# hT of two blocks in one tile and one load, loads earlier than the rows, and lists of four blocks in 16 pieces

## The chip, the cores and the metric

The kernel runs on one core of a Trainium2 chip. The metric is the device time of one execution in microseconds, lower is better. A core has five engines with a queue of instructions each: TensorE (PE in the profile, its weight loads PEld), VectorE (DVE), ScalarE (ACT), GpSimd (POOL) and SyncE (SP), which here only issues DMAs. The DMAs of all of them run on 16 DMA engines.

## The reference, cut to what matters

```python
# x: (16, 1024, 256); adj: (1024, 1024), sparse, some 9 nonzeros in a column; D = 256
pre_u = einsum('bud,dk->buk', h_t, W1[:d])
pre_v = einsum('bvd,dk->bvk', h_t, W1[d:])
hidden = relu(pre_u[:, :, None, :] + pre_v[:, None, :, :] + b1)
S = sigmoid(einsum('buvk,ko->buvo', hidden, W2)[..., 0] + b2[0])
a_t = einsum('buv,bud->bvd', S * A_a, h_t)
m_t = einsum('uv,bud->bvd', A_m, h_t) * h_t
z_t = beta1 * h_t + beta2 * (a_t @ Wa + ba) + beta3 * (m_t @ Wm + bm)
```

Both A_a and A_m are `adj`. Only edges (u, v) with a nonzero weight count, so the kernel builds lists of edges and gathers the rows of their sources.

## The kernel before, in words

**Tables and blocks.** The 16 batches are four groups g of GB = 4, and the 1024 nodes are eight tiles of 128. A block (g, vt) is one group and one tile of target nodes, so there are 32. For each group a table in DRAM has a row of 2048 numbers for each node: the four pre_u of the group, then its four h. `rows(k)` makes the first half for one tile of nodes: in two pieces TensorE multiplies hT, the transposed h, by W1's upper half (L384), ScalarE copies the product to `tab` (L400), and one step later SP stores it (L403). `copy_h` (L378) copies h itself from DRAM to DRAM. All rows of a group must be there before the first block of the group gathers.

**Lists.** `lists(vt)` makes the edges of a tile of targets: it loads 128 columns of adj (L238), turns nonzeros to keys (L244), takes the largest keys by maxima (L251 to L260), distributes the edges to slots with small matmuls (L270, L307), and matches slot and edge (L315 to L321). It ends with `uidx`, the sources to gather, `vidx`, where their weights lie, and `onehot`. It is a generator, and each `yield` is a place where it may be put off. The lists of tiles 0 to 3 are made mainly in the opening. Those of 4 to 7 (EARLY = 4) are advanced by the table `advance` while other blocks run. `fetch_val` (L341) then gathers the weights, two gathers of ten a step.

**The main loop.** A block has T = 10 steps, of 128 edge slots each, and the loop over n has 320. `fetch` (L453) gathers a slot's rows, one megabyte if all slots are used, into one of NF = 5 buffers, and is issued up to five steps ahead. `expand` (L523) brings pre_v to the slots with a 0/1 matrix. `gate` adds both (L539, 128x1024) and makes four relu-weighted sums (L543); ScalarE takes the sigmoid (L546) and scales the one-hot matrix with it (L549). `aggregate` (L560) sums h over edges on TensorE. At fixed steps s within a block, `half_end`, `turn_over` (L578, L581, L591) and `block_end` (L609 to L615) finish the block before, and `halves` prepares pre_v of the next one (L384, L420). VectorE's `times_h` (L591) is the last reader of a block's hT.

**Order.** The schedule is written by hand: every engine runs its instructions in the order in which the loop emits them. Blocks run in the order (0, 0..5), (1, 0..5), (0, 6..7), (1, 6..7), (2, 0..7), (3, 0..7). Rows of tiles 6 and 7 of groups 0 and 1 are needed long before their blocks, so their hT is loaded for the rows, given up, and loaded once more (`again`). The rows of the first eight blocks in `turn` are made in the opening; for others `plan` gives three steps each: that of the load and of the copy of h, and those of the two pieces of `rows`:

```python
plan([(2, vt) for vt in range(NT)], ((62 + 10 * i, 68 + 10 * i, 73 + 10 * i) for i in range(NT)))
```

**Buffers.** `hts` has ten buffers of 4 KB a partition, one for each block's hT; `hta` has three more, for blocks that are loaded twice. A load waits on SP's queue until its buffer's last reader is done. SP's queue also carries loads of h (L714), table stores (L403) and output stores (L615), in the order of the loop.

Of the kernel before, what the change touches and what calls it, by code (L numbers as in the profile page):

```python
# [7 lines left out]
FP = mybir.dt.float32  # L8
# [3 lines left out]
ALU = mybir.AluOpType  # L12
AX = mybir.AxisListType
P = 128
# [3 lines left out]
def kernel(  # L18
# [42 lines left out]
    nc = tc.nc  # L61
    B, N, D = x.shape
    NT = N // P
    DC = D // P
    GB = 4
# [21 lines left out]
    xT_rows = xT.rearrange("b (c p) n -> p (b c) n", p=P)  # L87
# [17 lines left out]
    def fixed(shape, name, dt=FP):  # L105
        return const.tile(shape, dt, name=name)
# [5 lines left out]
    ukey = fixed([P, N], "ukey")  # L112
# [96 lines left out]
    main = ctx.enter_context(ExitStack())  # L209
    gat = main.enter_context(tc.tile_pool(name="gat", bufs=1))  # L210
    one = main.enter_context(tc.tile_pool(name="one", bufs=1))
    big = main.enter_context(tc.tile_pool(name="big", bufs=2))
    hts = main.enter_context(tc.tile_pool(name="hts", bufs=NT + 2))
    hta = main.enter_context(tc.tile_pool(name="hta", bufs=3))
    wk = main.enter_context(tc.tile_pool(name="wk", bufs=3))
    psc = main.enter_context(tc.tile_pool(name="psc", bufs=2, space=bass.MemoryType.PSUM))
# [13 lines left out]
    EARLY = 4  # L230
# [3 lines left out]


    def lists(vt):
        key = fetched[vt + 1][:, :N] if vt < EARLY else big.tile([P, N], FP, name="key", bufs=1)
        (nc.sync if 2 <= vt < EARLY else nc.gpsimd).dma_start(key, adjT[vt * P:(vt + 1) * P, :])  # L238
        yield
# [1 line left out]
        top = R[:, 5:5 + S]  # L241
        count = wk.tile([P, 1], FP, name="count", bufs=4)
        unread = one.tile([P, N], mybir.dt.uint8, name="unread")
        nc.vector.scalar_tensor_tensor(key, key, 0.0, ukey, ALU.not_equal, ALU.mult)  # L244
        nc.scalar.activation(unread, key, AF.Sign, accum_out=count)
        yield

# [1 line left out]
        cand = wk.tile([P, N // P, 8], FP, name="cand", bufs=2)  # L249
        for c in range(N // P):  # L250
            nc.vector.max(cand[:, c, :], key[:, c * P:(c + 1) * P])  # L251
        yield
        cut = wk.tile([P, 1], FP, name="cut", bufs=2)
        nc.vector.tensor_reduce(cut, cand[:, :, 7], AX.X, ALU.max)
# [2 lines left out]
        for s in range(0, S, 8):  # L257
            nc.vector.max(top[:, s:s + 8], keys)
            if s + 8 < S:
                nc.vector.scalar_tensor_tensor(keys, keys, top[:, s + 7:s + 8], keys, ALU.is_lt, ALU.mult)  # L260

        used = wk.tile([P, S], FP, name="used", bufs=4)
        nc.vector.tensor_scalar(used, top, 0.0, None, ALU.is_gt, ALU.add, accum_out=R[:, 0:1])
# [29 lines left out]
        last = wk.tile([P, 1], FP, name="last", bufs=4)  # L293
        nc.vector.scalar_tensor_tensor(used, nth, held, top, ALU.is_equal, ALU.mult, accum_out=last)
        nc.vector.tensor_tensor(thr[:, vt:vt + 1], last, none, ALU.add)
        RR = wk.tile([P, NW, RC], FP, name="RR", bufs=2)
        few = wk.tile([P, E], mybir.dt.uint8, name="few", bufs=2)
        nc.scalar.copy(few, mark)
        for w, mine in enumerate((soon, late)):
            nc.vector.tensor_scalar(RR[:, w, :], R, mine, None, ALU.mult)  # L300
        yield
# [14 lines left out]
        eq = wk.tile([P, M, S], FP, name="eq", bufs=1)  # L316
        nc.vector.tensor_tensor(eq, nth.unsqueeze(1).to_broadcast([P, M, S]),
                                s_of.unsqueeze(2).to_broadcast([P, M, S]), ALU.is_equal)
        nc.vector.tensor_tensor(eq, eq, L[:, :, 5:], ALU.mult)
        k_of = wk.tile([P, M], FP, name="k_of", bufs=2)  # L320
        nc.vector.tensor_reduce(k_of, eq, AX.X, ALU.add)  # L321
        sl = slice(vt * NW, (vt + 1) * NW)
        nc.vector.tensor_scalar(uidx[:, sl].rearrange("p w j -> p (w j)"), k_of, -1.0, float(N), ALU.mult, ALU.add)
        nc.vector.tensor_tensor(k_of, L[:, :, 2], k_of, ALU.subtract)
# [43 lines left out]
    hTs = {}  # L368

    def load_hT(k):  # L370
        g, nt = k
        hTs[k] = hta.tile([P, GB, DC, P], FP, name="hT_") if k in again else hts.tile([P, GB, DC, P], FP, name="hT")
        nc.sync.dma_start(hTs[k].rearrange("p b c n -> p (b c) n"),
                          xT_rows[:, g * GB * DC:(g + 1) * GB * DC, nt * P:(nt + 1) * P])

    def copy_h(k, engine=nc.scalar):
        g, nt = k
        engine.dma_start(table[g][nt * P:(nt + 1) * P, GD:].rearrange("n (b d) -> n b d", b=GB),  # L378
                            x_rows[nt * P:(nt + 1) * P, g * GB:(g + 1) * GB, :])
# [64 lines left out]
    BS = NG * NT  # L444
# [15 lines left out]
    turn = [(g, vt) for g in range(2) for vt in (*range(FIRST, NT), *range(FIRST))]  # L460
    tabs = [fetched[0][:, :GD], *(f[:, GD:] for f in fetched)]
    for i in range(NT):
        if i < 2:
            next(made[i])
        load_hT(turn[i])
        if i in (5, 7):
            next(made[i // 2])
    COPIES = 2
# [5 lines left out]
    m = 0  # L474
# [37 lines left out]
    marks, pcs, accs, evs, hbs, LTs, lefts = {}, {}, {}, {}, {}, {}, {}  # L512
# [164 lines left out]
    begun = set(turn[:NT])  # L677
    end = parts = piece = last = None
    load_mark(0)
    for n in range(2):  # L680
# [3 lines left out]
    for n in range(total + 2):  # L684
        k, s = divmod(n, T)
# [25 lines left out]
        if s == 0 and 0 < k < BS:  # L711
            hbs[k - 1] = big.tile([P, GB, D], FP, name="h_blk", bufs=1)
            g, vt = order[k - 1]
            nc.sync.dma_start(hbs[k - 1], x_rows[vt * P:(vt + 1) * P, g * GB:(g + 1) * GB, :])  # L714
        if n == total - 6:
            hbs[BS - 1] = hts.tile([P, GB, DC, P], FP, name="hT").rearrange("p b c n -> p b (c n)")
            for v, m, f in tails:
                for h, o in tail_rows(x, v, m, f):
                    nc.sync.dma_start(h, o)
# [50 lines left out]
    with tc.If(any_left > 0):  # L770
        with ExitStack() as s2:
# [3 lines left out]
            for vt in range(NT):  # L775
# [3 lines left out]
                for b in range(B):  # L779
                    hT = fw.tile([P, DC, P], FP, name="fb_hT")  # L780
# [7 lines left out]
                key = fb.tile([P, N], FP, name="fb_key")  # L788
# [88 lines left out]
```

## Time and profile before

| | |
|---|---|
| time, median of 4 runs | 1196.73 us (1189.58 to 1200.31) |
| the profiled execution's own time | 1193.77 us |
| its span, first to last instruction | 1191.9 us |
| mean granted TensorE clock | 0.974 |
| busy: TensorE, weight loads, VectorE, ScalarE, GpSimd | 92%, 61%, 89%, 75%, 36% |
| DMA: moved, mean rate | 391.40 MB, 328 GB/s |
| opening, until the first L539 | 72.2 us |

The page gives busy time of each engine and share of 16 DMA engines by queue: q0 is GpSimd's, q1 SP's, q10 ScalarE's. A window row gives busy time and number of instructions of each engine in a stretch of time, then the granted clock, the share of 16 DMA engines and GB/s. A wait row names the engine and line that waited, what released it, the sum, the number and the longest. Busy time of TensorE is modelled, since its matmuls overlap.

### The profile page before, as it was taken

The page shows a single profiled execution, that of the slowest core. Times are in us where ns is not written, and L with a number is a line of the kernel's source. Part 1 is how long each engine was busy: PE and PEld are TensorE (multiplying, and loading weights), DVE is VectorE, ACT ScalarE, POOL GpSimd, SP SyncE. Part 2 cuts the span into 40 slices and gives each one's busy share as a digit, 9 for nine tenths or more (in the row PEclk, how much of TensorE's full clock was granted, in tenths as well). Part 3 has the DMA queues.
Part 4 walks back from the last instruction along what each step waited for, and adds up shares of the span by engine and source line. Part 5 has one row for each costly group of instructions (what it writes and reads, how often), then busy time and mean ns, then how long its engine had stood idle before and what let it go on. Part 6 is the DMA issues. An engine that isn't in the chain of part 4 may idle for free. (4 is left out here: it accounts for less than half of the span.)

```text
span 1191.9 us, 23914 instructions
## 1 busy us (share of the span) xinstructions
PE 1099.9 (92%) x7633; PEld 727.9 (61%) x7633; DVE 1065.1 (89%) x3483; ACT 897.6 (75%) x2624; POOL 432.8 (36%) x428
## 2 busy tenths in 40 slices
PE   7756989989899999999999999999999999999986
PEld 6643655656566665666666666666666666666653
DVE  8678979978999997999999889999999999999994
ACT  3347667768778767888888788888888888888873
POOL 1546762433253326323333333333333333333330
PEclk9878989999999989999999999999999999999999
DMA  9986799999989989999999999999999999999992
GB/s 290 289 288 217 256 346 349 319 329 341 322 285 344 381 279 314 365 373 379 375 358 351 348 335 364 365 369 382 357 362 351 356 317 327 327 334 332 329 342 88
DMA packets 147047, 391.40 MB, mean 328 GB/s; under 512 B 16752, under 2 KB 105328, under 8 KB 110704
## 3 DMA queue, kind: packets, MB, share of 16 engines
q0 software_dynamic: 50016, 300.50, 68.4%
q1 hardware_dynamic: 81616, 74.99, 19.6%
q10 hardware_dynamic: 15280, 14.29, 3.7%
q8 instruction: 63, 1.03, 0.3%
q14 instruction: 72, 0.59, 0.1%
HBM read 393.78 MB, written 50.33 MB: 373 GB/s over the span
## 5 line engine op out<-in xcount | busy, mean ns | idle before, releaser
L453 POOL DMA_INDIRECT fetched<-table,uidx x320 | 335.2, 1048 | 665.6 <-PE acc L560 512.0
L543 DVE SCALAR_TENSOR_TENSOR t<-t,w_b 128x256 f32<-128x256 f32 x1280 | 469.8, 422 | 22.0
L539 DVE TENSOR_TENSOR t<-fetched,pc 128x1024 f32<-128x1024 f32 x320 | 389.5, 1217 | 60.5 <-DMA fetched<-table,uidx 23.8
L560 PE MATMUL acc<-fetched,left 128*32 128x256 f32 x4096 | 340.1, 391 | 33.3 <-ACT left L549 23.7
L549 ACT ACTIVATE left<-left,gt 128x32 f32<-128x32 f32 (+1 forms) x1280 | 299.3, 304 | 10.4
L523 PE MATMUL pc<-X,mark 128*128 128x512 f32 x640 | 237.1, 452 | 14.3 <-DVE t L539 7.6
L560 PEld LDWEIGHTS acc<-fetched,left 128*32 128x32 f32 x4096 | 132.6, 109 | 181.9 <-issue 58.5
L523 PEld LDWEIGHTS pc<-X,mark 128*128 128x128 f32 x640 | 96.8, 190 | 148.9 <-issue 78.3
L546 ACT ACTIVATE gt<-sc,b_b 128x4 f32<-128x4 f32 x320 | 96.0, 300 | 59.3 <-DVE t L543 52.0
L384 PE MATMUL misc<-w_u,hT 128*128 128x256 f32 x448 | 111.0, 395 | 8.4 <-issue 3.6
L609 PE MATMUL misc<-w_m,LT 128*128 128x256 f32 x496 | 117.1, 379 | 0.0
L609 PE MATMUL misc<-w_a,LT 128*128 128x256 f32 x496 | 117.1, 379 | 0.0
L533 ACT ACTIVATE left<-onehot,val 128x128 f32<-128x128 bf16 (+1 forms) x320 | 116.6, 364 | 0.0
L384 PE MATMUL misc<-w_v,hT 128*128 128x256 f32 x448 | 108.4, 386 | 0.0
L543 DVE DVE_READ_ACCUMULATOR t<-t,w_b 128x1 f32 x1280 | 104.3, 82 | 0.0
L609 PEld LDWEIGHTS misc<-w_m,LT 128*128 128x128 f32 x496 | 94.0, 189 | 15.1
L609 PEld LDWEIGHTS misc<-w_a,LT 128*128 128x128 f32 x496 | 93.9, 189 | 15.0
L384 PEld LDWEIGHTS misc<-w_u,hT 128*128 128x128 f32 x448 | 87.9, 199 | 22.9 <-issue 3.7
L384 PEld LDWEIGHTS misc<-w_v,hT 128*128 128x128 f32 x448 | 86.7, 194 | 14.4
L341 POOL DMA_INDIRECT val<-in_adjT_dram,vidx x80 | 84.6, 1058 | 29.6 <-issue 20.7
L581 ACT COPY LT<-misc 128x512 f32<-128x512 f32 x128 | 70.9, 575 | 24.9 <-PE misc L578 6.3
L578 PE MATMUL misc<-ident,ev 128*128 128x128 f32 x512 | 74.2, 277 | 11.9 <-issue 7.1
(160 smaller groups left out, 898.9 us busy)
## 6 DMA issues: line engine op xcount, KB each, us to landing
h_blk<-in_x_dram SPq DMA_DIRECT2D x31, 512.0 KB
out_dram<-z SPq DMA_DIRECT2D x31, 512.0 KB
hT<-in_xT_dram SPq DMA_DIRECT2D x28, 512.0 KB
table<-tab SPq DMA_DIRECT2D x26, 512.0 KB
table<-in_x_dram ACTq DMA_DIRECT2D x24, 512.0 KB
fetched<-table,uidx POOLq DMA_INDIRECT x320
table<-in_x_dram SPq DMA_DIRECT2D x8, 512.0 KB
table<-fetched SPq DMA_DIRECT2D x6, 512.0 KB
```

Of the source, the lines that this page charges most:

```text
L341: nc.gpsimd.indirect_dma_start(out=val[:, i, j:j + 1], out_offset=None, in_=adj_flat, in_offset=bass.IndirectOffsetOnAxis(ap=vidx[:, i, j: ...
L384: nc.tensor.matmul(p[:, bb * D:(bb + 1) * D], hT[:, 2 * h + bb, i, :], wt[:, i, :], start=(i == 0 and not begun), stop=(i == DC - 1), skip ...
L453: nc.gpsimd.indirect_dma_start(out=fetched[n % NF], out_offset=None, in_=table[g], in_offset=bass.IndirectOffsetOnAxis(ap=uidx[:, vt * NW ...
L523: nc.tensor.matmul(pcs[n][:, c], marks[n // TW][:, j * P:(j + 1) * P], cuts[k][:, w, c], start=True, stop=True)
L533: nc.scalar.activation(lefts[n][:, :m, :, 0, :], onehot[:, i, o:o + m, :].unsqueeze(2).to_broadcast([P, m, GB, V]), AF.Copy, scale=val[:, ...
L539: nc.vector.tensor_tensor(t, fetched[n % NF][:, :GD].rearrange("p (b d) -> p b d", b=GB), pcs.pop(n).rearrange("p (b d) -> p b d", b=GB), ...
L543: nc.vector.scalar_tensor_tensor(t[:, b, :], t[:, b, :], 0.0, w2_b, ALU.max, ALU.mult, accum_out=sc[:, b:b + 1])
L546: nc.scalar.activation(gt, sc, AF.Sigmoid, bias=b2_b)
L549: nc.scalar.activation(lefts[n][:, :m, b, 1, :], lefts[n][:, :m, b, 0, :], AF.Copy, scale=gt[:, b:b + 1])
L560: nc.tensor.matmul(accs[h][b * 2 * V:(b + 1) * 2 * V, r, :], left[:, i, b].rearrange("p k v -> p (k v)"), f[:, GD + b * D:GD + (b + 1) * D ...
L578: nc.tensor.transpose(pt[:, i * P:(i + 1) * P], ev[:, r, c * P:(c + 1) * P], ident)
L609: nc.tensor.matmul(pz[:, bb * D:(bb + 1) * D], LTs[k][:, c, 2 * h + bb, i, :], wt[:, c, :], start=False, stop=(i == 0 and c == DC - 1), sk ...
```

## The change

1. hT of two neighbouring blocks (g, 2i) and (g, 2i+1) lies in one tile, 256 columns in place of 128, and comes by one DMA. `hts` has NT / 2 + 1 = 5 buffers of 8 KB. The first pair alone is loaded by two DMAs. Only the second loads of tiles 6 and 7 in groups 0 and 1 use `hta`, and the h of the last block does, which took an `hts` buffer before.
2. The steps in `plan` are others: most loads stand eight steps or more ahead of the first piece of rows, and the first step now is that of the copy of h, with the load only where the pair isn't loaded yet. The pieces stand at other steps of a block.
3. The lists of tiles 4 to 7 are advanced in 16 pieces, one a step from the fourth step on, after the load; before, there were nine, in 14 steps. L244 is halved for these. They start at steps 0, 19, 48 and 88; before, at 0, 20, 50 and 80.

```diff
-    hts = main.enter_context(tc.tile_pool(name="hts", bufs=NT + 2))
+    hts = main.enter_context(tc.tile_pool(name="hts", bufs=NT // 2 + 1))
...
+        fine = vt >= EARLY
...
-        nc.vector.scalar_tensor_tensor(key, key, 0.0, ukey, ALU.not_equal, ALU.mult)
+        if fine:
+            nc.vector.scalar_tensor_tensor(key[:, :N // 2], key[:, :N // 2], 0.0, ukey[:, :N // 2],
+                                           ALU.not_equal, ALU.mult)
+            yield
+        rest_ = slice(N // 2 if fine else 0, N)
+        nc.vector.scalar_tensor_tensor(key[:, rest_], key[:, rest_], 0.0, ukey[:, rest_], ALU.not_equal, ALU.mult)
...
             nc.vector.max(cand[:, c, :], key[:, c * P:(c + 1) * P])
+            if fine and c == N // P // 2 - 1:
+                yield
...
+            if fine and s == 8:
+                yield
...
         nc.vector.tensor_tensor(thr[:, vt:vt + 1], last, none, ALU.add)
+        if fine:
+            yield
...
                                 s_of.unsqueeze(2).to_broadcast([P, M, S]), ALU.is_equal)
+        if fine:
+            yield
         nc.vector.tensor_tensor(eq, eq, L[:, :, 5:], ALU.mult)
         k_of = wk.tile([P, M], FP, name="k_of", bufs=2)
         nc.vector.tensor_reduce(k_of, eq, AX.X, ALU.add)
+        if fine:
+            yield
...
-    def load_hT(k):
+    def load_hT(k, apart=False):
         g, nt = k
-        hTs[k] = hta.tile([P, GB, DC, P], FP, name="hT_") if k in again else hts.tile([P, GB, DC, P], FP, name="hT")
-        nc.sync.dma_start(hTs[k].rearrange("p b c n -> p (b c) n"),
-                          xT_rows[:, g * GB * DC:(g + 1) * GB * DC, nt * P:(nt + 1) * P])
+        if k in begun:
+            t = hta.tile([P, GB, DC, P], FP, name="hT_")
+            blocks = [k]
+        else:
+            t = hts.tile([P, GB, DC, 2 * P], FP, name="hT")
+            blocks = [k, (g, nt + 1)]
+        n = P * len(blocks)
+        for c in range(0, n, P) if apart else (0,):
+            m = P if apart else n
+            nc.sync.dma_start(t.rearrange("p b c n -> p (b c) n")[:, :, c:c + m],
+                              xT_rows[:, g * GB * DC:(g + 1) * GB * DC, nt * P + c:nt * P + c + m])
+        for i, k in enumerate(blocks):
+            hTs[k] = t[:, :, :, i * P:(i + 1) * P]
+            begun.add(k)
...
-    for i, n in zip(range(EARLY, NT), (0, 20, 50, 80)):
-        for o in (0, 4, 5, 6, 7, 9, 11, 13, 15, 17):
+    for i, n in zip(range(EARLY, NT), (0, 19, 48, 88)):
+        for o in (0, *range(4, 20)):
             advance[n + o] = (*advance.get(n + o, ()), i)
...
-    plan(turn[NT:], ((0, 5, 8), (6, 12, 15), (12, 18, 22), (17, 25, 28), (24, 32, 35), (31, 38, 42), (38, 45, 48),
-                     (43, 50, 52)))
-    plan([(2, vt) for vt in range(NT)], ((62 + 10 * i, 68 + 10 * i, 73 + 10 * i) for i in range(NT)))
-    plan([(3, vt) for vt in range(NT)], ((146, 152, 157), (156, 162, 167), *((153 + 10 * i, 158 + 10 * i, 161 + 10 * i)
-                                                                             for i in range(2, NT))))
+    plan(turn[NT:], ((0, 8, 11), (5, 12, 15), (7, 18, 21), (12, 23, 25), (24, 32, 35), (31, 38, 41), (44, 51, 52),
+                     (46, 53, 54)))
+    plan([(2, vt) for vt in range(NT)], ((64, 72, 73), *((60 + 10 * i, 68 + 10 * i, 71 + 10 * i) for i in range(1, NT))))
+    plan([(3, vt) for vt in range(NT)], ((135, 149, 151), (147, 158, 161), (183, 191, 194), (188, 198, 201),
+                                         (203, 211, 214), (208, 218, 221), (223, 231, 232), (225, 233, 234)))
...
         if n in loads:
-            load_hT(loads[n])
-            if loads[n] not in begun:
+            if loads[n] not in copied:
                 copy_h(loads[n])
-                begun.add(loads[n])
+                copied.add(loads[n])
+            if loads[n] not in hTs:
+                load_hT(loads[n])
```

More of the change, by code (lines that the diff above doesn't have):

```diff
@@ L367 @@
     order += [(g, vt) for g in range(2, NG) for vt in range(NT)]
-    hTs = {}
-    def load_hT(k):
+    hTs, begun = {}, set()
+    def load_hT(k, apart=False):
         g, nt = k
-        hTs[k] = hta.tile([P, GB, DC, P], FP, name="hT_") if k in again else hts.tile([P, GB, DC, P], FP, name="hT")
-        nc.sync.dma_start(hTs[k].rearrange("p b c n -> p (b c) n"),
-                          xT_rows[:, g * GB * DC:(g + 1) * GB * DC, nt * P:(nt + 1) * P])
+        if k in begun:
[12 more added lines that the diff above has]
+            begun.add(k)
     def copy_h(k, engine=nc.scalar):
@@ L464 @@
             next(made[i])
-        load_hT(turn[i])
+        if i % 2 == 0:
+            load_hT(turn[i], i == 0)
         if i in (5, 7):
@@ L669, in plan @@
             at.update((n, k) for n in pieces)
-    plan(turn[NT:], ((0, 5, 8), (6, 12, 15), (12, 18, 22), (17, 25, 28), (24, 32, 35), (31, 38, 42), (38, 45, 48),
-                     (43, 50, 52)))
-    plan([(2, vt) for vt in range(NT)], ((62 + 10 * i, 68 + 10 * i, 73 + 10 * i) for i in range(NT)))
-    plan([(3, vt) for vt in range(NT)], ((146, 152, 157), (156, 162, 167), *((153 + 10 * i, 158 + 10 * i, 161 + 10 * i)
-                                                                             for i in range(2, NT))))
+    plan(turn[NT:], ((0, 8, 11), (5, 12, 15), (7, 18, 21), (12, 23, 25), (24, 32, 35), (31, 38, 41), (44, 51, 52),
[3 more added lines that the diff above has]
+                                         (203, 211, 214), (208, 218, 221), (223, 231, 232), (225, 233, 234)))
     plan(again, ((103,), (113,), (125,), (133,)))
-    begun = set(turn[:NT])
+    copied = set(turn[:NT])
     end = parts = piece = last = None
@@ L715 @@
         if n == total - 6:
-            hbs[BS - 1] = hts.tile([P, GB, DC, P], FP, name="hT").rearrange("p b c n -> p b (c n)")
+            hbs[BS - 1] = hta.tile([P, GB, DC, P], FP, name="hT_").rearrange("p b c n -> p b (c n)")
             for v, m, f in tails:
```

## The prediction

> **What bounds the kernel now.** I first read the page's totals: VectorE is busy 89% of the span, TensorE 92%, the 16 DMA engines 68.4 + 19.6 + 3.7 = 92% on the three queues that carry data. Three resources that close together mean that no total decides. So I cut the span by stages: a step is one L539 add, its start times come from the tile view of `t`, and ten steps are a block. The busy time by window, from the opening to the tail:
>
> ```profile
> core 0: us, PE busy (x) PEld busy (x) DVE busy (x) ACT busy (x) POOL busy (x), PEclk, DMA share, GB/s
> 0.00:72.20 72.20, 48.41 (x211) 41.83 (x212) 50.45 (x227) 25.75 (x42) 24.91 (x38) 0.86 0.94 297
> 72.20:159.20 87.00, 68.46 (x427) 43.77 (x427) 74.76 (x253) 53.61 (x157) 57.45 (x55) 0.87 0.78 253
> 159.20:235.60 76.40, 73.10 (x506) 49.93 (x505) 71.01 (x240) 58.33 (x169) 32.00 (x31) 0.99 0.94 335
> 235.60:316.00 80.40, 72.13 (x511) 47.77 (x510) 66.86 (x221) 59.33 (x174) 28.15 (x29) 0.98 0.92 328
> 316.00:531.10 215.10, 205.29 (x1404) 135.91 (x1404) 196.44 (x643) 165.35 (x486) 83.69 (x82) 0.98 0.94 336
> 531.10:730.60 199.50, 194.20 (x1375) 127.22 (x1374) 181.56 (x572) 164.07 (x485) 63.76 (x61) 1.00 0.97 358
> 730.60:922.80 192.20, 190.59 (x1383) 125.56 (x1381) 181.12 (x572) 163.39 (x486) 60.49 (x60) 1.00 0.99 364
> 922.80:1142.20 219.40, 211.73 (x1515) 134.85 (x1515) 211.05 (x667) 184.55 (x554) 74.92 (x71) 1.00 0.92 332
> 1142.20:1191.90 49.70, 36.02 (x310) 21.05 (x308) 31.81 (x100) 23.24 (x78) 7.40 (x7) 0.96 0.56 191
> ```
>
> The rows after the opening are blocks 0-1, 2-3, 4-5, 6-11, 12-17, 18-23, 24-30 and 31. Blocks 24-30, where nothing but gathers and the block's own work is left, give the floor: 219.4 / 7 = 31.3 us a block with VectorE busy 30.2. Blocks 0-23 take 850.6 us, 99 above 24 such floors (751). Four lists explain about 42 of the 99: VectorE's busy time is 36.35 in block 8 and 34.48 in block 9 against 30.24 in block 12, so one list costs 10.4 us. Some 57 us are stalls, and the waits of VectorE between 72 and 923 us name them:
>
> ```profile
> DVE t L539 <- DMA fetched<-table,uidx: 23.4, 24, 3.1
> DVE t L539 <- PE pc L523: 14.4, 11, 2.7
> DVE t L539 <- remote: 4.4, 3, 2.4
> ```
>
> So gathers that come late are the largest. Where and why is seen in single blocks, 8, 9, 10 and 12:
>
> ```profile
> 385.90:424.60 38.70, 35.00 (x232) 23.18 (x224) 36.35 (x127) 28.16 (x83) 10.84 (x11) 0.91 0.95 349
> 424.60:460.20 35.60, 35.45 (x260) 23.35 (x258) 34.48 (x117) 28.47 (x83) 15.96 (x15) 1.00 0.85 292
> 460.20:497.20 37.00, 34.64 (x237) 22.80 (x232) 30.26 (x97) 27.93 (x83) 15.96 (x17) 1.00 0.99 350
> 531.10:563.30 32.20, 31.61 (x219) 21.07 (x221) 30.24 (x96) 26.61 (x80) 10.34 (x10) 1.00 1.00 376
> ```
>
> Blocks 8 and 9 make a list and VectorE sets them, with DMA at 0.85 in block 9; block 10 makes none, VectorE idles 6.7 us, and DMA is at 0.99. The two limits alternate instead of overlapping. GpSimd is a third. For five steps after each list it issues two gathers of `val` ahead of each gather of rows:
>
> ```profile
> 236.24 1.00 POOL L453 DMA_INDIRECT fetched<-table,uidx  x1 [0.30 <-issue]
> 237.54 1.00 POOL L341 DMA_INDIRECT val<-in_adjT_dram,vidx  x1 [0.30 <-issue]
> 238.84 1.01 POOL L341 DMA_INDIRECT val<-in_adjT_dram,vidx  x1 [0.30 <-issue]
> 240.15 0.99 POOL L453 DMA_INDIRECT fetched<-table,uidx  x1 [0.30 <-issue]
> ```
>
> That is 3 x 1.30 = 3.9 us a step, above 3.13, and in steps 1 to 20 it goes on without a break: it, not DMA (0.78), sets blocks 0-1.
>
> **What the Trainium skill says.** "DMA: Bandwidth & Descriptors", section "Issuing engines are not separate DMA queues": DMAs issued by any engine end up on the same 16 engines. The trace agrees, the three queues' shares add up to 92%, so a load of hT is paid by the gathers. Same page, "Why small descriptors are slow (HBM only)": each packet carries a fixed overhead. The trace's packet records agree: 512-byte packets of hT take 29 ns on the mean, 1024-byte ones 50 ns, so two halves cost 58. "Perfetto Trace Analysis", section "What 'DMA-bound' means": the issuing sequencer can be the limit; the GpSimd rows above show it. Same page, section "Optimization Strategy": with regimes that differ in their most contended engine, interleaving them can pay. Blocks 8 to 10 are that case.
>
> **The change part by part.**
>
> *One load for two blocks.* 1024 packets of 1 KB replace 2 x 1024 of 512 bytes: 2048 x 29 / 16 = 3.7 us of 16 engines becomes 1024 x 50 / 16 = 3.2, so 0.5 us a pair. Fifteen of 16 pairs are whole, 7.5 us of DMA, of which three pairs lie in the opening. There TensorE first reads the third block at 17.3 us, while the fourth block has landed by 15.1 (packet records), so waiting for a pair costs the opening nothing; and what it waits for later are lists (7.2 us on R at 64), so it gains nothing either. TensorE reads the same number of columns, VectorE's L591 the same elements. SBUF stays 40 KB a partition for the pool.
>
> *When loads start.* A pair's buffer is free only after both blocks. So two hT and a copy of h (512 KB, 1.55 us) start together at steps 24, 44, 64, 80, 100, 120, 135, 183, 203 and 223, and the other copy alone some steps later. Before, one hT and one copy started together, 1.85 + 1.55 = 3.4 us; now 3.2 + 1.55 = 4.75. On SP's queue the load waits for L591 of the block just ended; behind it stand only the next z store, h_blk load and table store, none of which is due within the same step. Copies now stand ahead of loads, on ScalarE's queue, and wait for nothing.
>
> *Finer lists.* No operation is new but the halves of L244: from 1219 ns at 1024 elements and 285 at 64 (L260) a half is 0.72, so 0.22 us more a list, under 0.9 us in all, one third of it behind other limits. The largest pieces were the eight maxima (1.64), cut to R (2.18), mark to thr and RR (about 2.6) and the matching (2.1); now about 1.5 and 2.0. Each list goes on for 16 steps in place of 14, and list 7 starts at step 88, not 80.
>
> *Sum by stage, against the profiled execution (1193.8 us; span 1191.9).*
> - Blocks 0-1: a step with a piece over 0.9 us (3.9 - 3.02 of VectorE's own) is late. Before: (1.64 - 0.9) + (2.18 - 0.9) + (2.6 - 0.9) + (2.1 - 0.9) = 4.9. After: (1.5 - 0.9) + (2.0 - 0.9) = 1.7. Minus 3; bounds 0, if a lead of buffers covers it, and -5. The two pairs loaded here (6.4 us) find DMA idle for 0.22 x 87 = 19 us.
> - Blocks 2-3: 3.3 us of hT for (1,0) and (1,1) have moved ahead of them. VectorE needs 71 + 2 of 76.4, so at most -3 is there; I take -1, bounds -3 and +2.
> - Blocks 4-5: the val steps 37 to 41 lose a load and a copy (3.4 us) from under them, and steps 44 to 46 get two hT and two copies, 6.3 us. VectorE waits 7 us in steps 41 to 47 now. I take 3 off and 2 on: -1, bounds -5 and +4.
> - Blocks 6-11: about half of list 7, 5 us, falls into block 10, where VectorE idles 6.7 us. Block 8 loses its list. -5, bounds -9 (the sum of VectorE's floors with lists is 188 + 16 = 204 of 215, and 2 stay) and +1.
> - Blocks 12-17: one hT and one copy fewer, and four hT at the pair's price: 194 of DMA becomes 189.5, the floor is 187.8. Rows no longer stand at s = 2 and 7, where TensorE's L384 waited twice for 1.3 us on ScalarE's LT. 199.5 becomes 192.5: -7, bounds -10 and -2.
> - Blocks 18-23: one hT and one copy more, pairs cheaper: +1.9 of DMA on 190, so DMA is above the floor throughout: +3, bounds 0 and +9. The last table store goes out at step 235, one step before the first gather of group 3 is issued; that gather is used 14 us later, which I count at nothing.
> - Opening and tail: nothing.
>
> Sum: -3 -1 -1 -5 -7 +3 = -14, so 1180 on the profiled execution, which stood 3 us below the median of 1196.7: **1182**.
>
> **Rivals.** *The gain is lost (within 1%).* The bytes are the same and the loop's DMA is busy 797 of 850 us; if DMA's idle time cannot be filled because five buffers limit the lead, only the packets' saving in stages at 0.97 and above remains, about 4 us: 1192. For it: blocks 18-23 are already at 0.99. Against it: blocks 8 to 10 above.
> *Slower: the pair as a burst.* The place is L539 in steps 24-28, 44-48 and after each later pair. A gather is issued 9.3 us before its use (steps 270 to 300) and takes 2.5 us of all engines; 4.75 us of other packets between two gathers, shared in turn, can use up that lead, and at a DMA share of 0.95 or more it does not come back within the block. Were each of the ten loads to cost 2.5 us, that is +25 against the -8 of lists (stages 0-1 and 6-11): 1197 + 17 = 1214. It decides once a pair adds more than about 2 us of wait on gathers. For it: 3.1 us at step 103, right behind two loads. Against it: blocks 18-22, with 3.4 us at once, wait 1.3 us at most.
> *Better.* If every stage comes to within 2 us a block of its floor, the bounds above are reached: about -26, 1171.
> That the loads are not merged is excluded by the instruction order: the built program has 15 loads of 128x8x256.
>
> **How the numbers follow.** Forecast 0.42, lost gain 0.30, slower 0.14, better 0.14. The forecast's own range is 1172 to 1192. A measurement of this kernel tells about 1% (12 us) from no change. Faster by over 1%: 0.14 + 0.8 x 0.42 = 0.48. Slower: 0.14. Within: 0.38, the lost gain and the near tail of the forecast. The range reaches from 1163 to 1203; beyond it lie the far ends of the last two cases.
>
> **What would show it.** Right: block 10 with VectorE busy near 35 and its length near 37, block 8 near 33, blocks 12-17 near 192, blocks 18-23 at 194 to 197 with a DMA share of 0.99, the 512-byte packets mostly gone, the wait on gathers below 23 us. Wrong: waits of L539 on gathers right after the ten pair loads; blocks 18-23 over 201; or blocks 0-1 unchanged at 87, which would say that GpSimd alone sets them.

## The result, and the profile after

| | before | after |
|---|---|---|
| median | 1197.56 us (63 runs, 1189.45 to 1216.89) | 1196.45 us (42 runs, 1189.22 to 1204.32) |
| profiled execution: time, span | 1193.77, 1191.9 us | 1196.74, 1194.7 us |

The ratio is 0.9993 with a 95% interval of 0.9978 to 1.0008. The forecast was 14 us faster; this comparison shows no gain.

The busy time by stage (the same stages as before the change, cut at the starts of L568, which is L539 of before; columns: PE, PEld, DVE, ACT, POOL busy, granted clock, DMA share, GB/s):

```profile
72.40:161.10 88.70, 74.81 (x438) 48.30 (x441) 74.04 (x254) 53.11 (x158) 52.94 (x53) 0.85 0.78 257
161.10:239.90 78.80, 72.47 (x498) 49.43 (x495) 70.65 (x241) 57.86 (x168) 33.06 (x33) 0.98 0.89 312
239.90:317.60 77.70, 73.69 (x508) 48.99 (x510) 66.66 (x222) 57.86 (x173) 30.47 (x30) 1.00 0.89 333
317.60:532.70 215.10, 199.59 (x1409) 131.55 (x1402) 196.10 (x645) 165.12 (x487) 86.83 (x83) 1.00 0.94 339
532.70:726.60 193.90, 190.47 (x1369) 124.76 (x1368) 181.20 (x571) 162.18 (x484) 62.70 (x61) 1.00 0.98 362
726.60:924.60 198.00, 194.90 (x1378) 129.09 (x1377) 181.39 (x571) 163.08 (x484) 62.85 (x60) 1.00 0.96 357
```

Blocks 0-1 are no shorter (88.7 against 87.0), blocks 2-3 neither (78.8, 76.4), blocks 6-11 are equal (215.1). Blocks 12-17 gained 5.6 us, and blocks 18-23 gave 5.8 back. VectorE's busy time is within 0.8 us of before in every row, so nearly all that moved is idle time. Single blocks, 8 to 10:

```profile
388.80:423.00 34.20, 33.65 (x250) 22.20 (x251) 30.25 (x97) 28.30 (x84) 12.18 (x12) 1.00 1.01 380
423.00:460.50 37.50, 35.41 (x253) 23.35 (x251) 36.20 (x127) 30.22 (x90) 12.74 (x12) 1.00 0.91 332
460.50:497.20 36.70, 31.12 (x211) 21.20 (x212) 34.51 (x117) 24.38 (x70) 15.92 (x16) 1.00 0.96 337
```

Half of list 7 did fall into block 10's idle time: VectorE is busy 34.5 us there instead of 30.3, in a block of the same length. Block 8 lost its list and 4.5 us. But blocks 7, 9 and 11 became 1.4, 1.9 and 1.6 us longer (35.7, 37.5 and 35.5 us), which takes it back. The waits of VectorE from 72 to 925 us:

```profile
DVE t L568 <- DMA fetched<-table,uidx: 19.7, 22, 3.1
DVE t L568 <- PE pc L552: 13.7, 13, 2.5
DVE s_of L327 <- ACT L L323: 7.6, 2, 6.6
DVE t L568 <- remote: 6.0, 3, 4.5
```

Gathers are waited for 3.7 us less (23.4 before). A new wait of 6.6 us stands at step 15 in L327 (the matching of a list, L315 of before). The waits on `remote`, a release whose source the profile doesn't name, have grown too; most of it is one wait of 4.5 us at step 44. How it came about can be read from GpSimd's rows before it ("..." stands for rows left out; the last line is VectorE's own row):

```profile
236.31 1.29 POOL L481 DMA_INDIRECT fetched<-table,uidx  x1 [0.97 <-PE misc L607]
237.90 1.00 POOL L357 DMA_INDIRECT val<-in_adjT_dram,vidx  x1 [0.30 <-issue]
239.20 1.07 POOL L357 DMA_INDIRECT val<-in_adjT_dram,vidx  x1 [0.30 <-issue]
240.57 1.00 POOL L481 DMA_INDIRECT fetched<-table,uidx  x1 [0.30 <-issue]
241.87 0.99 POOL L357 DMA_INDIRECT val<-in_adjT_dram,vidx  x1 [0.30 <-issue]
243.17 0.99 POOL L357 DMA_INDIRECT val<-in_adjT_dram,vidx  x1 [0.30 <-issue]
245.42 1.00 POOL L481 DMA_INDIRECT fetched<-table,uidx  x1 [1.26 <-PE pc L552]
...
251.39 1.00 POOL L481 DMA_INDIRECT fetched<-table,uidx  x1 [0.31 <-issue]
...
259.64 1.22 DVE L568 TENSOR_TENSOR t<-fetched,pc 128x1024 f32<-128x1024 f32 x1 [4.47 <-remote]
```

The rows' gathers (L481) are issued at 236.31, 240.57, 245.42 and 251.39, that is 4.3, 4.9 and 6.0 us apart, where a step needs 3.1: the two gathers of `val` take 2.6 us in between, and on top of them comes any wait for a free buffer. The gather of step 44 was issued at 251.39, and VectorE stands until 259.64. Spacing is not all of it: SP issued a table store at 251.81 and the load of a pair at 252.19, which shared the DMA engines with this gather. Before the change, waits of this kind stood at steps 41 to 43, and after the other lists at 71 to 74 and at 101 to 103. Now the last one is at 114 (3.1 us), because the `val` of list 7 is gathered at steps 106 to 112 in place of 96 to 102.

### The profile page after: what moved, and what is told of

Its sections match the earlier page's. It is cut to its first block, busy times and chain, and to the rows that moved or that the text cites. A ratio compares the mean times of both kernels' runs of the same rounds, so it can differ in the third digit from the quotient of the medians.

```text
span 1194.7 us, 23882 instructions
## 1 busy us (share of the span) xinstructions
PE 1101.7 (92%) x7633; PEld 728.9 (61%) x7633; DVE 1063.6 (89%) x3487; ACT 893.2 (75%) x2624; POOL 437.4 (37%) x428
## 5 line engine op out<-in xcount | busy, mean ns | idle before, releaser
L481 POOL DMA_INDIRECT fetched<-table,uidx x320 | 341.3, 1067 | 663.5 <-PE acc L589 512.7
L568 DVE TENSOR_TENSOR t<-fetched,pc 128x1024 f32<-128x1024 f32 x320 | 389.4, 1217 | 60.9 <-DMA fetched<-table,uidx 24.1
L578 ACT ACTIVATE left<-left,gt 128x32 f32<-128x32 f32 (+1 forms) x1280 | 299.3, 304 | 10.4
L589 PEld LDWEIGHTS acc<-fetched,left 128*32 128x32 f32 x4096 | 135.8, 109 | 192.1 <-ACT left L578 60.7
L412 PE MATMUL misc<-w_u,hT 128*128 128x256 f32 x512 | 124.9, 391 | 15.7 <-DMA hT<-in_xT_dram 7.0
L412 PEld LDWEIGHTS misc<-w_u,hT 128*128 128x128 f32 x512 | 97.9, 196 | 30.5 <-DMA w_u<-in_W_dram 5.8
L597 ACT COPY ev<-acc 128x512 f32<-128x512 f32 x128 | 75.7, 591 | 9.9 <-PE acc L589 4.4
```

The source lines that it names most:

```text
L412: nc.tensor.matmul(p[:, bb * D:(bb + 1) * D], hT[:, 2 * h + bb, i, :], wt[:, i, :], start=(i == 0 and not begun), stop=(i == DC - 1), skip ...
L481: nc.gpsimd.indirect_dma_start(out=fetched[n % NF], out_offset=None, in_=table[g], in_offset=bass.IndirectOffsetOnAxis(ap=uidx[:, vt * NW ...
L568: nc.vector.tensor_tensor(t, fetched[n % NF][:, :GD].rearrange("p (b d) -> p b d", b=GB), pcs.pop(n).rearrange("p (b d) -> p b d", b=GB), ...
L578: nc.scalar.activation(lefts[n][:, :m, b, 1, :], lefts[n][:, :m, b, 0, :], AF.Copy, scale=gt[:, b:b + 1])
L589: nc.tensor.matmul(accs[h][b * 2 * V:(b + 1) * 2 * V, r, :], left[:, i, b].rearrange("p k v -> p (k v)"), f[:, GD + b * D:GD + (b + 1) * D ...
L597: nc.scalar.copy(evs[q], accs.pop(q))
```

## The experiments

The theory to be tested: the pairs, the early loads and the pieces do what they should, but GpSimd's two gathers of `val` a step hold the stages in which they should have paid. Rivals: the finer lists bring a loss of their own (the wait at step 15); the rows of group 3, bunched at 191 to 234, give back what blocks 12-17 gain; the sum of DMA bytes bounds all.

Kernels of one group ran on one chip and share its runs of the kernel before. That kernel took 1179, 1181 and 1179 us in groups 1, 4 and 5, and 1198 in groups 2 and 3, so times are compared within a group only. Groups 1 and 2 have the same chip number in the record, so the difference need not be one of chips. Most expectations were written against a kernel of 1197 us and miss the absolute times of the faster groups for that reason. Each median is of 6 to 22 runs, that of e16 of two; the ratios are the record's and need not be the quotient of two medians.

| group | kernel | median us | ratio to before, 95% interval |
|---|---|---|---|
| 1 | e1_lists_only | 1181.40 | 1.0004 [0.9978, 1.0029] |
| 1 | e2_loads_only | 1171.93 | 0.9947 [0.9927, 0.9967] |
| 1 | e3_val1 | 1165.40 | 0.9871 [0.9834, 0.9909] |
| 1 | e4_copy_first | 1171.89 | 0.9924 [0.9904, 0.9943] |
| 2 | e6_after_again | 1194.45 | 0.9966 [0.9943, 0.9990] |
| 2 | e7_single_loads | 1196.56 | 0.9983 [0.9963, 1.0004] |
| 2 | e8_single_g3 | 1193.74 | 0.9963 [0.9937, 0.9990] |
| 3 | e9_after_control | 1197.32 | 0.9989 [0.9967, 1.0010] |
| 3 | e10_copy_first_2 | 1197.00 | 0.9988 [0.9960, 1.0016] |
| 3 | e11_val1_cf | 1166.24 | 0.9742 [0.9701, 0.9784] |
| 3 | e12_coarse_val1 | 1167.91 | 0.9751 [0.9709, 0.9792] |
| 4 | e13_before_val1 | 1174.62 | 0.9959 [0.9934, 0.9984] |
| 4 | e14_val1_again | 1165.27 | 0.9882 [0.9842, 0.9922] |
| 4 | e15_single_val1 | 1167.32 | 0.9890 [0.9852, 0.9927] |
| 4 | e16_no_z | 1162.49 | 0.9853 [0.9790, 0.9915] |
| 5 | e17_spread | 1165.23 | 0.9880 [0.9853, 0.9908] |
| 5 | e18_best | 1156.17 | 0.9801 [0.9772, 0.9829] |

The length of the stages, worked out from the starts of the L539 adds (L568 in the changed kernel) of each profiled execution (us):

```
steps           before   e5   e13 |  after   e6   e9 |   e4   e10 |  e11   e14   e16   e17   e18
0-20              87.0  87.4  77.9 |  88.7  86.5  88.8 |  78.0  85.1 |  76.4  77.8  77.8  79.3  76.5
20-40             76.4  77.4  74.8 |  78.8  81.0  77.4 |  75.8  78.4 |  75.2  73.0  73.0  74.0  74.5
40-60             80.4  76.1  73.9 |  77.7  76.1  77.9 |  74.3  77.7 |  72.7  71.4  71.2  72.0  71.4
60-120           215.1 214.3 207.6 | 215.0 214.7 216.9 | 211.1 221.5 | 207.9 208.6 208.5 208.8 207.9
120-180          199.5 200.2 200.2 | 193.9 193.8 194.9 | 192.8 193.3 | 192.9 192.8 194.3 194.6 193.8
180-240          192.2 202.4 201.6 | 198.0 198.3 197.0 | 196.8 196.4 | 196.4 196.8 197.0 197.6 191.6
240-250           31.6  31.3  31.4 |  33.3  33.2  34.5 |  34.2  34.3 |  34.3  34.4  32.1  33.2  32.0
```

The three kernels on the left have before's plan of loads, and e13 has one gather of `val` a step besides. The next three are the changed kernel. Then comes one variant of it in two groups (e4 and e10), and on the right are variants with one gather of `val` a step. Two profiles of before, or two of the changed kernel, differ by up to 4.3 us in a stage of steps 0 to 60, so smaller differences there mean nothing.

**The two halves apart: lists alone and loads alone.** e1 is before with the finer pieces and new starts of the lists; e2 is the changed kernel with the old pieces and starts (cut to the table of steps).

```diff
-    for i, n in zip(range(EARLY, NT), (0, 19, 48, 88)):      # e2: and fine = False
-        for o in (0, *range(4, 20)):
+    for i, n in zip(range(EARLY, NT), (0, 20, 50, 80)):
+        for o in (0, 4, 5, 6, 7, 9, 11, 13, 15, 17):
```

> The kernel before with the finer lists and their new starts (0, 19, 48, 88) alone; loads and rows as before. The forecast's own view: blocks 0-1 at 84 and blocks 6-11 at 210, about 1188 in all. Rival (GpSimd): the stall after a list belongs to the ten gathers of weights that GpSimd issues two a step ahead of the gathers of rows, so it moves with the list (from steps 101 and 103 to 111 and 114) and blocks 6-11 stay at 215; the matching of list 4 waits some 6 us for ScalarE's copy L, which stands behind four DMA issues, so blocks 0-1 stay at 87 to 89; in all 1194 to 1199. Both expect blocks 12-17 at 199 and 18-23 at 192, as before.

> The changed kernel with lists of 4 to 7 in the pieces and at the steps of before; pair loads and the new plan stay. If the loads account for what changed late: blocks 12-17 at 194 (199.5 before), blocks 18-24 at 231 (224 before), a sum of about 0 to +2 there, and blocks 0-11 as before but for list waits; 1195 to 1199 in all. If the pairs alone gave a loss that the lists made good: 1200 or more. If they gave a gain that the lists ate: 1192 or less.

The lists alone are worth nothing (1.0004). The loads alone are worth 7 us in this group (0.9947), where the kernel before takes 1179. So what gain there is comes from the loads.

**One gather of `val` a step.** e3 is the changed kernel with one edit in the main loop.

```diff
-            fetch_val(2)
+            fetch_val(1)
```

> The changed kernel with one gather of weights a step in place of two, so ten steps for a list in place of five. GpSimd theory: with 2.6 us of issues a step in place of 3.9 GpSimd no longer sets blocks 0-1 (88.7 to 80 or less), and VectorE's waits at steps 41 to 44, 71 to 74 and 111 to 114 (some 18 us now) fall under 6; 1180 to 1188 in all. DMA theory (the bytes set it, the issue rate does not): no change, 1194 to 1198.

It is the fastest of group 1, 6.5 us below loads alone. In group 3, where the kernel before takes 1198, the same edit is worth far more, as shown below.

**The new wait at step 15.** In `lists` ScalarE issues four stores to `whose` (L316) ahead of the copy L (L323) for which L327 waits. e4 puts the copy first.

```diff
-        for w in range(NW): ... dma_start(whose[...], few[...])
         pe = aside(vt)
...
         nc.scalar.copy(L.rearrange(...), pe[...])
+        for w in range(NW): ... dma_start(whose[...], few[...])
         yield
```

> The changed kernel with ScalarE's copy L (L323) put in front of the four DMA issues of whose in the same piece. The 6.6 us of VectorE's wait at step 15 go. If that wait is on the path: blocks 0-1 fall from 88.7 to 83 to 85 and the time by 4 to 6 us, to 1191. If GpSimd's issues set these blocks: they stay at 87 or more and the time at 1196.

It came out at 1171.89, like loads alone (1171.93; the intervals of the two ratios overlap). This doesn't yet tell whether the copy was worth anything, since the changed kernel itself was not in group 1; e10 does, below.

**Both kernels once more, with single loads, and with before's steps for group 3.** e5 is a profile of before, e6 of the changed kernel. e7 keeps the changed plan but loads each hT singly (512 KB, ten buffers); e8 is e7 with group 3's rows from step 178 on at one block in ten steps, each load five steps ahead, as before.

```diff
-        t = hts.tile([P, GB, DC, 2 * P], FP, name="hT"); blocks = [k, (g, nt + 1)]
+        hTs[k] = hts.tile([P, GB, DC, P], FP, name="hT")          # e7, bufs=NT + 2
...
+    plan(..., *((153 + 10 * i, 158 + 10 * i, 161 + 10 * i) for i in range(2, NT)))   # e8
```

> The kernel before, once more, for its stages on another chip: if stages differ from chip to chip more than between kernels, blocks 0-5 will differ from 87, 76 and 80 by several us; blocks 24-30 at 31.3 each on any chip.

> The changed kernel, once more. If the wait at step 15 for ScalarE's copy belongs to the kernel: VectorE waits again 3 to 7 us for L there. If it was chance: under 1 us. Blocks 18-24 at 229 to 232 in any case, since rows of four blocks stand late.

> The changed kernel with a 512 KB load for each hT into ten buffers as before; steps of rows, copies and lists as changed, each load at the step of its copy. If what pairs save in packets (0.5 us of DMA a pair, 7.5 in all) matters: 3 to 6 us above the changed kernel. If a pair as a burst costs as much: equal within 2 us. If the burst costs more: 3 us or more below.

> As the run with single loads, but rows of group 3 one block in ten steps from step 178 on, as before the change, which pairs with five buffers do not allow. If lateness of these rows is what blocks 18-24 lose: they fall from some 230 to 224 and the time by 5 to 7 us against the run with single loads. If it is the number of bytes alone: no change, since the same bytes move.

The three ratios overlap: neither the pair nor this place of group 3's rows is worth what could be told apart (pair against single: 2 us; e8 against e7: 3 us). e5 brought something else. Its steps 180 to 240 took 202.4 us, where before's own profile had 192.2. TensorE stood for a load of hT (first the wait row, then the load's issue on SP, then the matmul that used it):

```profile
PE misc L384 <- DMA hT<-in_xT_dram: 7.1, 2, 5.8
```

```profile
737.37 0.37 SPq L373 DMA_DIRECT2D hT<-in_xT_dram  x1
```

```profile
753.62 0.73 PE L523 MATMUL pc<-X,mark 128*128 128x512 f32 x2
760.16 2.47 PE L384 MATMUL misc<-w_u,hT 128*128 128x256 f32 x5 [5.81 <-DMA hT<-in_xT_dram]
```

A load of 512 KB issued at 737.37 could be used at 760.16 only, 22.8 us later; before's plan starts it five steps (16 us) ahead. The same stands in e1 (7.8 us the longest) and in e13:

```profile
PE misc L384 <- DMA hT<-in_xT_dram: 6.4, 2, 5.3
```

It stands in none of the three profiles of the changed kernel, which loads hT seven steps or more ahead of its rows; of its variants, e12, e8, e17 and e15 have one wait of 2.1, 1.6, 0.9 and 0.4 us. The profile of before that I predicted from had none of these waits.

**The wait at step 15 and the gathers of `val`, where before takes 1198.** e9 is the changed kernel, e10 repeats e4, e11 is e10 with `fetch_val(1)`, e12 is e2 with `fetch_val(1)`.

> The changed kernel beside the next three on one chip. Theories: (L) the finer lists lose what they gain to VectorE's wait for the copy L; (G) GpSimd's two gathers of weights a step cost 8 us and more whatever the lists are; (D) DMA bytes alone set the loop, and none of these edits matters. A ratio of 0.996 to 0.999 to the kernel before, as in the two comparisons so far.

> The changed kernel with the copy L in front of the four DMA issues, again, now beside the changed kernel itself. L: 4 to 8 us (0.3 to 0.7%) below it. G: within 2 us of it, since GpSimd holds blocks 0-1. D: no difference.

> The changed kernel with both, copy L first and one gather of weights a step. G and L together: the gains add to 12 to 18 us below the changed kernel, a ratio of 0.983 to 0.988. If both end the same wait: no better than one gather a step alone (0.987). D: 0.997.

> The changed kernel with lists in the old pieces at the old steps, and one gather of weights a step. G: 8 us and more below the same with two (0.9947 measured), so 0.986 to 0.988. If finer lists help once GpSimd is relieved: 3 us or more above the run with both edits. If they do not: equal to it within 2 us.

The copy first gives nothing (0.9988 against 0.9989), so the new wait is not on the path. One gather of `val` a step takes 31 us off (1197.0 to 1166.2), about twice what was expected. By the stages of e10 and e11, all of it lies in steps 0 to 120 (462.7 to 432.2 us). TensorE's granted clock is no rival there: in blocks 0-1 it was 0.92 in e10 and 0.93 in e11, at 85.1 and 76.4 us. Fine and coarse lists are equal with it (0.9742, 0.9751), so the pieces are worth nothing even when GpSimd has room: this part of the theory is refuted.

**The kernel before with one gather of `val`, single loads with it, and the output stores taken away.** e13 is before with `fetch_val(1)`, e14 repeats e3, e15 is e7 with `fetch_val(1)`. e16 is e14 without the stores of z in blocks 12 to 23, so it leaves that part of the output unwritten.

```diff
+        if not 12 <= k < 24:          # e16
             after(step + 3, lambda: nc.sync.dma_start(out[...], z))
```

> The kernel before, with one gather of weights a step in place of two and nothing else. If GpSimd held it back as it did the changed kernel: 1163 to 1172 us. If the change itself is worth the forecast's 14 us once GpSimd is relieved: 1178 to 1182, against 1166 of the changed kernel. If the change is worth nothing: 1164 to 1168. A load of hT five steps ahead may land late in some executions (5.8 and 7.8 us of TensorE seen), which would add 0 to 8.

> The changed kernel with one gather of weights a step, beside the other three on one chip: 1164 to 1168, a ratio of 0.974 on a chip where the kernel before takes 1198, 0.987 where it takes 1179.

> As e14, with hT in 512 KB loads of one block each into ten buffers. If the packets saved by pairs count where DMA is the limit: 2 to 6 us above e14. If not: within 2 us. If the burst of a pair costs: 2 us or more below.

> As e14, with the output stores of blocks 12 to 23 left out (those parts of the output stay unwritten): 12 x 1.6 = 19 us of DMA less between steps 120 and 250, which take 425 us against a floor of 13 x 31.3 = 407. If DMA holds this stage: 407 to 414. If something else does (issue, TensorE): 420 or more.

e14 in the same stages as above, blocks 0-1, 2-3 and 4-5, and its waits of VectorE from 72 to 927 us:

```profile
71.60:149.50 77.90, 69.36 (x447) 45.30 (x449) 73.60 (x255) 54.22 (x159) 41.20 (x40) 0.93 0.86 299
149.50:222.50 73.00, 69.90 (x490) 47.84 (x482) 70.52 (x241) 57.26 (x168) 41.96 (x41) 1.00 0.93 332
222.50:293.90 71.40, 70.84 (x512) 47.30 (x510) 66.67 (x222) 58.57 (x174) 35.77 (x34) 1.00 0.97 364
```

```profile
DVE t L568 <- DMA fetched<-table,uidx: 16.8, 19, 3.0
DVE t L568 <- PE pc L552: 7.9, 8, 2.0
```

VectorE's busy time is that of the changed kernel (73.6, 70.5, 66.7), and the stages are 10.8, 5.8 and 6.3 us shorter than in the result's profile; that one is of another set of runs, so e10 and e11 are the comparison within a group. DMA's share rises from 0.78, 0.89 and 0.89 to 0.86, 0.93 and 0.97: the transfers were held back at their issue. Over these six blocks GpSimd has as many instructions as in the changed kernel (115 and 116); what counts is how many stand between two gathers of rows.

With one gather of `val` in both, the change is worth 9.3 us (1174.62 to 1165.27, ratio 0.9920); no expectation had named 1174.62. By stages, steps 120 to 250 give all of it: 433.2 us in e13, 424.0 in e14. Steps 120 to 180 give 7.4 and steps 180 to 250 1.8. But the first profile of before, where no hT came late, took 423.3 us in steps 120 to 250, as much as e14: without late loads, what the change gains in blocks 12-17 it loses behind them. What is left is the late hT, 6.4 us of TensorE's waits in e13. This is argued from one undisturbed profile, not shown by an experiment. Pairs against single loads: 1165.27 and 1167.32, not told apart. e16, steps 120 to 180 and 180 to 240:

```profile
499.50:693.80 194.30, 191.49 (x1382) 125.53 (x1374) 181.29 (x572) 162.76 (x485) 64.33 (x61) 1.00 0.96 352
693.80:890.80 197.00, 194.44 (x1373) 128.83 (x1371) 181.74 (x572) 162.36 (x481) 63.52 (x60) 1.00 0.93 342
```

Twelve stores of 512 KB are gone. At the 1.55 us that a copy of that size takes, they are an estimated 19 us of 16 engines; by the shares in steps 120 to 250 (0.97 in e14, 0.94 in e16) it was some 13. DMA falls from 0.96 to 0.93 in steps 180 to 240, and the stage is as long as with them (196.8); steps 120 to 250 together take 423.4 us against 424.0. So in this profile the sum of bytes doesn't bound them.

**Bursts.** Left were the short clashes: a pair of hT, a copy of h and a store in one or two steps, and rows at 231 to 234. e17 is e14 with the eight copies of h of group 3 at steps 145, 150, ... 180, away from the loads. e18 is e17 with the copy L first, hT of (3, 2) and (3, 3) loaded singly into `hta`, and group 3's rows spread:

```diff
+    early = {145 + 5 * i: (3, i) for i in range(NT)}          # e17 and e18: copy_h(early[n])
...
-    plan([(3, vt) for vt in range(NT)], ((135, 149, 151), (147, 158, 161), (183, 191, 194), (188, 198, 201),
-                                         (203, 211, 214), (208, 218, 221), (223, 231, 232), (225, 233, 234)))
+    plan([(3, vt) for vt in range(NT)], ((135, 149, 151), (147, 158, 161), (157, 168, 171), (166, 178, 181),
+                                         (187, 198, 201), (197, 208, 211), (206, 218, 221), (217, 228, 231)))
```

> The changed kernel with one gather of val a step, and the eight copies of h of group 3 moved to steps 145, 150, ... 180, so that in steps 183 to 225 a load of hT no longer starts together with a copy of h. Theory of bursts: the waits on gathers right after steps 183, 203 and 223 shorten, blocks 20, 22, 23 and 24 fall from 137 us together to about 131, and the time from 1165 to about 1160. Rival (these steps are held by something else, or the copies cost the same wherever they are): steps 120 to 250 stay at 423 to 427 us, the time at 1164 to 1167.

> e17_spread with the copy of L ahead of the four stores to whose, tiles 2 and 3 of group 3 loaded singly into hta, and the rows of group 3 spread over steps 149 to 231, at most one load in ten steps, none at steps 232 to 234. If bursts and the bunched last rows are what steps 180 to 250 lose: 1155 to 1160, with steps 120 to 250 at about 417. If not: 1164 to 1167, as without it.

Copies alone do nothing (1165.23). The spread plan does: 1156.17, 9 us less, ratio to before 0.9801 [0.9772, 0.9829], the fastest here. Steps 120 to 180 and 180 to 240 of e18, and VectorE's waits from 700 to 930 us, first of e14, then of e18:

```profile
501.30:695.10 193.80, 192.70 (x1392) 127.59 (x1392) 181.22 (x571) 164.00 (x486) 62.67 (x60) 1.00 1.01 383
695.10:886.70 191.60, 189.88 (x1378) 124.52 (x1371) 180.86 (x571) 162.78 (x485) 61.29 (x61) 1.00 0.96 351
```

```profile
DVE t L568 <- DMA fetched<-table,uidx: 8.6, 7, 3.0
DVE t L568 <- PE pc L552: 3.4, 5, 1.2
```

```profile
DVE t L568 <- DMA fetched<-table,uidx: 4.3, 8, 1.1
...
DVE t L568 <- PE pc L552: 0.5, 1, 0.5
```

Two more blocks' rows in steps 120 to 180 cost nothing there (193.8, DMA 1.01), and without them steps 180 to 250 fall from 231.2 in e14 to 223.6: the waits on gathers and on TensorE's `pc` both shrink. Which of e18's edits did it was not tried singly. Single loads (e15) and the copy L first (e10) were worth nothing by themselves, so the new steps of group 3's loads and rows are the likeliest. But e8 had spread these rows too, with two gathers of `val` a step, loads five steps ahead and fewer rows before step 180, and gained nothing that could be told apart, so it is open what about the steps counts.

## Why the prediction was wrong

Most of the signs that I had named for "right" came out: block 10 with VectorE busy 34.5 us, block 8 at 34.2, blocks 12-17 at 193.9, the wait on gathers at 19.7. The time stood still all the same. The signs named the places where the gain should appear, and not those where it could be lost.

**Blocks 0-1 (-3 forecast; 86.5 to 88.8 measured against 87.0 and 87.4).** The step that failed is the list of late steps, 4.9 us before and 1.7 after: it counts every piece over 0.9 us as a loss. I had found that GpSimd needs 3.9 us a step there and then took VectorE's pieces off on top of it. The size of the pieces is worth nothing in either case: not with two gathers of `val` a step (e1, 1.0004), and not with one (e11 with fine lists 76.4 us, e12 with coarse ones 77.0). The bound of "0, if a lead of buffers covers it", was the right term; that the buffers are the reason is not shown. My own sign, "unchanged at 87, which would say that GpSimd alone sets them", came out in its first half only. GpSimd is the lever (85.1 us in e10, 76.4 in e11), yet not alone: its rows' gathers came every 3.9 to 5.3 us in nearly all steps of the changed kernel's blocks 0-1, where 3.9 is its own work and the rest is mostly a wait for a buffer. In e4, in a group where before takes 1179, they came every 4.0 to 4.3 in most steps, and the stage took 78.0. The two add up because they stand in one queue. The Trainium skill's "Perfetto Trace Analysis", section "What 'DMA-bound' means", has the issuing sequencer as a possible limit; I quoted it and showed the rows for it, and did not ask which of my other gains it voids.

**Blocks 2-5 (-2; between -1.5 and +3.6 measured).** The changed kernel took 155.3 to 157.1 us, before 156.8 and 153.5. That is within the spread of profiles.

**Blocks 6-11 (-5; 0 measured).** The half list moved into block 10 as forecast, and block 8 came down as forecast. The step that failed is that nothing else was thought to move. Block 9 got more of the list (VectorE busy 36.2 us, 34.5 before) and became about as much longer. The ten gathers of `val` that go with list 7 came ten steps later, and the waits behind them moved from block 10 to block 11. Why block 7 became 1.4 us longer is not shown. With one gather of `val` a step the stage does fall by 6.4, but it falls in e13 too, which has the old lists.

**Blocks 12-17 (-7; -5.6 measured).** Right in place and nearly in size, but partly by luck, since most of the sum was DMA bytes. The loads give this gain (e2 193.4 us, e1 201.1), but neither the pair's price (193.6 with single loads in e15) nor fewer bytes: without six of the stores the stage took 194.3 (e16), with two more blocks' rows and loads 193.8 (e18). The other term fits, the rows away from s = 2 and 7: this wait of before (below) is gone in the changed kernel, and VectorE's waits on `pc` in the stage fall from 4.3 to 1.0 us. It was not tried by itself.

```profile
PE misc L384 <- ACT LT L581: 2.6, 2, 1.3
```

**Blocks 18-23 and 24 (+3 and 0; +5.8 and +1.7 measured).** Against the profile that I predicted from, the sign was right and the term too small. Its reason, "DMA is above the floor throughout", was wrong: e16 took bytes away and changed nothing, e18 moved loads and rows and won 7.6 us in steps 180 to 250. I dismissed block 24 with "that gather is used 14 us later"; VectorE waited there for a gather at step 241 (2.0 us in the changed kernel, 3.0 in e14). The bunched last rows are not the whole reason: with the same rows block 24 took 34.4 us in e14, but 31.9 in e7 and 32.1 in e16.

**What was missing.** Earlier loads were priced only as bursts; that they keep hT from being late was put at nothing. The profile of before didn't show it, since that execution had none of these waits. Three other profiles of before's plan have them (e1, e5, e13), and their steps 180 to 240 took 203.7, 202.4 and 201.6 us against 192.2, some 10 us more. Measured against these, steps 180 to 240 of the changed kernel (197.0 to 198.3) became shorter by 3 to 7 us, not longer by 6. So a gain existed, in part for another reason: steps 120 to 250 took 433.9 us in e5 and 425.3 and 426.4 in e6 and e9. Where it went in groups 2 and 3 is not fully shown. Steps 0 to 120 took 455.2 in e5 and 458.4 and 461.0 in e6 and e9, which would be about half of it, but the first profile of before had 458.9. The rival "gain is lost" had the right number. Its cause, the lead that five buffers limit, is at most a part: waits for a buffer are there, but the issue of gathers in the same queue, which it did not name, is what e11 took away.

**Left open.** Why the kernel before needs 18 us more in some groups is not settled. The same kernel (e4, e10) took 1171.89 and 1197.00; its two profiles differ by 7.1, 2.6, 3.4 and 10.4 us in the stages up to step 120 and by less than 1 us in any after it, and with one gather of `val` a step the variants of the changed kernel, e16 and e18 aside, agree across groups to 3 us (1165.2 to 1167.9). That shows where, not what. TensorE's clock alone doesn't explain it: in blocks 0-1 it was 0.87 in e2, at 78.9 us, and 0.92 in e10, at 85.1.

## What to carry to other kernels

When an in-order queue issues both urgent transfers and others that have time, count what stands between two urgent ones: one gather of 1.3 us more in each step cost 6.5 us in groups 1 and 4 and 31 us of 1197 in group 3, though the engine was busy only 37%. A gain on an engine counts only if no other limit holds the stage at the same time; take that limit away and measure the change again. Here the change then gave 9 us, where it had given 1 and 4 us in groups 2 and 3, and the finer lists gave nothing either way. And profile the kernel before more than once: a load that comes late in some executions only doesn't appear in one profile, and what a change does for it cannot be forecast from it.

## What was not expected of the hardware

A load of 512 KB on SP's queue, issued while the DMA engines were busy, could be used only 22.8 us after its issue in one case, where its bytes are worth 1.85 us of all 16 engines. Its packet records show a long tail: 938 of 1024 packets had started by 747.0, 10 us after the issue, and the last ended at 759.4, after 22 us. The five-step lead (16 us) was enough in the first profile of before. In contrast, 13 to 19 us of DMA work taken from steps 120 to 250, at a share of 0.97, did nothing for their length: here a share near 1 was no proof that bytes were the limit.
